# Graph network on one core: earlier node batches, the second last chunk normed in halves, a moved memory pool

## The chip, the cores and the metric

The kernel runs on one NeuronCore of a Trainium2 chip. The core has a matrix engine (PE; its weight loads are shown as PEld), a vector engine (DVE), an engine for activation functions (ACT), GpSimd (POOL), and a sync engine (SP) that here does nothing but issue DMAs. Each engine takes its own instructions in order, and they meet by semaphores. The metric is the time of one execution in microseconds, lower is better. Times are those of the device.

## The reference, cut to what matters

The input is a graph of 6250 nodes with 128 features and 200,000 edges. The edges are sorted by their destination `dst`; their sources `src` are random. One block of a graph network is added to the input:

```python
def mesh_conv(x, src, dst, ea, w1, b1, g, bt, w2, b2):
    m = concatenate([x[dst], x[src], ea], axis=-1) @ w1 + b1
    m = silu(group_norm(m, g, bt))                   # groups of 16 channels, per edge
    m = m @ w2 + b2
    return segment_sum(m, dst) / clip(count(dst), 1)[:, None]

h = relu(layernorm(x))
h = silu(group_norm(mesh_conv(h, ...first...), n1_g, n1_b)) + (silu(t_emb) @ tm_w + tm_b)
h = silu(group_norm(mesh_conv(h, ...second...), n2_g, n2_b)) + relu(layernorm(x))
q, k, v = h @ qw + qb, h @ kw + kb, h @ vw + vb      # 8 heads of 16
logits = (q[dst] * k[src]).sum(-1) / 4 + (ea @ ew + eb)
w = softmax of logits over the edges of each dst
o = segment_sum(w * v[src], dst) @ ow + ob
return x + h + group_norm(o, an_g, an_b)
```

So there are three sweeps over all edges: first convolution, second convolution, attention. Each needs for every edge a row that belongs to its source, and each sweep can start only when the node work of the sweep before is complete, since a source can be any node.

## The kernel before, in words

**Tiling.** Edges are taken 128 at a time (a tile), 8 tiles to a chunk of 1024 edges. There are 1563 tiles, so 196 chunks numbered 0 to 195, and the last chunk has only 3 tiles. Nodes are taken in 49 windows of 128. As the edges are sorted, one chunk touches a short run of nodes, and the sum of a chunk is added to two neighbouring windows of a table `flat` (named `U` in the convolutions) that stays on chip.

**One chunk of a convolution.** POOL gathers the source rows from a table `b_d` in memory, one indirect DMA for each of the 8 tiles (L718). SP loads a block of destination rows `pk` (L676) and, for two chunks at a time, a copy of the edges' positions spread over the partitions, `ohT` (L660). ACT turns `ohT` into a one-hot matrix in two passes (`compared`, L685 and L686). PE multiplies the two (`hidden`, L1174). DVE adds the gathered rows (`first`, L1181), ACT squares, DVE sums the squares of each group (L1185), ACT takes the root (L1192), and DVE the reciprocal (L1282). `normed` then does three passes on DVE (times the reciprocal L1196, times gamma L1199, plus beta L1200) and the Silu on ACT (L1201). `summed` (L1206) adds the edges up by destination on PE. `by_window` (L1211) makes two masked copies of that sum on ACT, one for each of the two windows, and `add_late` (L1216) adds them to `U` on DVE.

**Steps.** `pipeline` (L829) writes out one step per chunk. In step n the gathers of a chunk ahead are issued, chunk n gets its `first`, and an earlier chunk gets `normed` and `summed`. For one run of chunks there is one root; runs are two chunks long and become single chunks at the end. The last step takes chunks 194 and 195 together. The order on DVE, ACT, PE and SP is the order in which this function writes the instructions down, held by `in_order`; POOL is not held by it and goes ahead as far as its buffers allow (4 in the convolutions, 11 in attention).

**Batches.** While a sweep runs, windows that no later chunk touches are finished four at a time by a batch (`conv_nodes`, L950; a generator that does a little in each step). A batch divides by the count, multiplies by the second weight, normalises, takes the Silu, and multiplies by the weights of the next sweep; results go to the tables `b_d`, `a_d` (destination rows) and `kv_d` (keys and values). `plan_batches` (L375) says at which steps batches start: for the convolutions from step 81 on, every 8 steps, so 14 batches, the last at step 185. Which windows a batch takes is read from a small table that is computed on the chip from the edges. `idle` makes a batch wait some steps between its reciprocal and its transpose (6 in the first convolution, 4 in the second); the last batch of a sweep has none. In the first convolution the transpose and the Silu (`turned`, L909) stand in one step, and so do each product with the next weights and the copy of its result (L1006 and L1015).

**Ends of a sweep.** After the last chunk, `mend` (L745) reads two numbers; unless some edges or windows were left out, it does nothing, but all engines meet there. Then `last_nodes` (L1105) finishes the last 9 windows in three groups of three. Its tiles come from a pool `lastn`. Only then can the gathers of the next sweep read their table. Memory of pools that were closed is given to new pools, and the framework places the waits that this needs.

**Attention** has the same shape: gathers of keys and values (L718 on `kv_d`), products (L1384), logits (L1399 to L1405), maxima over runs of chunks for the softmax (loads of `nbs` and `nbe`, L1412), weighted sums (L1457, L1464) that are merged into `flat`.

Of the kernel before, what the change touches and what calls it, by code (L numbers as in the profile page):

```python
# [21 lines left out]
P = 128  # L22
# [7 lines left out]
G = 8  # L30
GC = 2
BN = 4
LG = 2
WN = 96
RN = 92
# [15 lines left out]
def kernel(ctx: ExitStack, tc: tile.TileContext, x, src, dst, eat, w, out):  # L51
# [323 lines left out]
    def plan_batches(i):  # L375

        ends, todo = steps_of(i)
        out, done = [], 0
        for n, now in enumerate(todo):
            done += len(now)  # L380
            if n % 8 == (4 if i == 3 else 1) and n > (40 if i == 3 else 80) and n + 6 < NCH \
                    and (i == 3 or n + 5 in ends):
                out.append((n, max(done - 3, 0)))
        return out if NWD else []
# [509 lines left out]
    class Nodes:  # L894
# [11 lines left out]
                nc.tensor.transpose(tp[:, j, :], t[:, j, :], ident)  # L906
            return tp[:, :m, :]

        def turned(self, t, m, tag="x", silu=None):  # L909

            tp = self.in_bank(t, m)
            out = self.tile(m, tag)
            if silu:
                nc.scalar.activation(out, tp, AF.Silu, bias=cols[f"{silu}_b"], scale=cols[f"{silu}_g"])
            else:
                nc.scalar.copy(out, tp)
            return out

        def times(self, tT, m, rhs):
# [27 lines left out]
    def span(w, m):  # L947
        return bass.ds(w, m) if not isinstance(w, int) else slice(w, w + m)

    def conv_nodes(b, i, w, m, idle=0, last=False):  # L950


        at = span(w, m)
# [23 lines left out]
        if i == 1 or last:  # L977
            b.inverse(A, m)
            h0T = b.in_bank(h0[:, at, :], m) if i == 2 else None
            yield  # L980
            for _ in range(idle + 2 * (idle > 0)):
                yield
            tT = b.turned(A, m, "t", silu=f"n{i}")
            if i == 2:
                nc.vector.tensor_tensor(tT, tT, h0T, ALU.add)
        else:
            b.scaled(A, m, f"n{i}_g", f"n{i}_b")
            yield
            nc.scalar.activation(A, A, AF.Silu)
# [14 lines left out]
        done = None  # L1004
        for rhs, bias, d_ in ends:
            o = b.times(tT, m, rhs)  # L1006
            if bias:
                yield
            if done:
                nc.sync.dma_start(out=rows_of(done[0], w, m), in_=done[1])  # L1010
            t = b.tile(m, "o")
            if bias:
                nc.vector.tensor_tensor(t, o, rows[bias][:, None, :].to_broadcast([P, m, D]), ALU.add)
            else:
                nc.scalar.copy(t, o)  # L1015
                yield
            done = d_, t
# [86 lines left out]

    def last_nodes(i, hx=True):  # L1105

        with tc.tile_pool(name="lastn", bufs=1) as lp, tc.tile_pool(name="lastp", bufs=6, space=PSUM) as ps:
# [28 lines left out]
    def conv(i):  # L1136
# [6 lines left out]
        with ExitStack() as es:  # L1143
# [23 lines left out]
            def over_edges(r, n):  # L1167
                return r[:, None, :].to_broadcast([P, n, D])
# [23 lines left out]
                nc.scalar.activation(sd[:, :n + also], var[:, :n + also], AF.Sqrt, bias=eps_t, scale=1.0 / HD)  # L1192
                return sd

            def normed(k):
                nc.vector.tensor_tensor(  # L1196
                    k.mt.rearrange("p t (g c) -> p t g c", c=HD), k.mt.rearrange("p t (g c) -> p t g c", c=HD),
                    k.rs.rearrange("p (t g) -> p t g", g=H)[:, :, :, None].to_broadcast([P, k.nt, H, HD]), ALU.mult)
                nc.vector.tensor_tensor(k.mt, k.mt, over_edges(gam, k.nt), ALU.mult)  # L1199
                nc.vector.tensor_tensor(k.mt, k.mt, over_edges(bet, k.nt), ALU.add)  # L1200
                nc.scalar.activation(k.mt, k.mt, AF.Silu)  # L1201

            def summed(k):
                k.u = ps_.tile([P, 3, PITCH], FP, name="u", tag="u", bufs=2)
# [13 lines left out]
            class Stage:  # L1218
# [506 lines left out]
```

## Time and profile before

| | us |
|---|---|
| median of 3 runs | 6132.63 |
| lowest and highest of them | 6124.32 and 6134.92 |
| the profiled execution, whole | 6127.41 |
| its span, first to last instruction | 6125.2 |

| engine | busy, us | share of the span |
|---|---|---|
| DVE | 4995.8 | 82% |
| POOL | 4498.1 | 73% |
| PE | 3621.9 | 59% |
| ACT | 3339.8 | 55% |

The profile has a timeline of every instruction with its start and duration, and, in brackets, how long its engine sat idle before it and which instruction of another engine ended that idle time. Groups of instructions are put together by source line; `x392` is their number, and the mean duration is in nanoseconds. The list of waits says for each pair of lines how long one waited for the other: the total, how many times, and the longest. "issue" is time in which an engine waited for nothing that the profile shows. A DMA on SP is shown at the time of its issue; "landing" is when its semaphore arrives. PEclk is the granted clock of PE, as a share of full speed.

### The profile page before, as it was taken

The numbers are of one execution on the slowest core, as the hardware profiler recorded it, in microseconds if no ns is written. First come the engines' busy times: TensorE is split into PE (matmuls) and PEld (weight loads), VectorE is DVE, ScalarE is ACT, GpSimd is POOL, SyncE is SP. The second block draws the span as 40 slices with busy tenths as digits, with TensorE's granted clock in tenths as the row PEclk, the third lists the DMA queues.
The fourth block names the chain that finished last, engine by engine and source line by source line (L and its number), as shares of the span: only waits on it lengthen the run. The fifth ranks groups of instructions, "written<-read, shape, count | busy, mean of one in ns | idle before, by whom it ended". The sixth has DMA issues, their size and how long they took to land. (4 is left out here: it accounts for less than half of the span.)

```text
span 6125.2 us, 68319 instructions
## 1 busy us (share of the span) xinstructions
PE 3621.9 (59%) x20941; PEld 3430.7 (56%) x20942; DVE 4995.8 (82%) x7118; ACT 3339.8 (55%) x5259; POOL 4498.1 (73%) x4738
## 2 busy tenths in 40 slices
PE   5565556565566455655566566655665665666665
PEld 4555555555555455555555555544555555555555
DVE  7888888888888587787888888866778888888887
ACT  5666666666666566666666666642333333333354
POOL 5777777777777577777777777757777777777774
PEclk8777777777777677776777777766777778777777
DMA  6444343444444333434444444445566666666653
GB/s 162 117 127 119 98 115 101 108 108 104 106 102 105 83 97 101 101 96 101 107 108 111 111 114 109 115 112 156 152 160 166 163 164 167 161 164 163 161 160 82
DMA packets 391220, 758.86 MB, mean 124 GB/s; under 512 B 89647, under 2 KB 256946, under 8 KB 361441
## 3 DMA queue, kind: packets, MB, share of 16 engines
q0 software_dynamic: 175056, 410.03, 26.1%
q1 hardware_dynamic: 210144, 340.73, 21.2%
q10 hardware_dynamic: 5632, 3.50, 0.2%
q8 instruction: 173, 2.83, 0.2%
q14 instruction: 215, 1.76, 0.1%
HBM read 707.34 MB, written 46.58 MB: 123 GB/s over the span
## 5 line engine op out<-in xcount | busy, mean ns | idle before, releaser
L718 POOL DMA_INDIRECT g<-b_d,src_i x3126 | 2965.1, 949 | 963.1 <-issue 917.4
L1206 PE MATMUL u<-h,oh 128*128 128x129 f32 (+1 forms) x6252 | 1282.2, 388 | 1424.2 <-ACT h L1201 1424.1
L1206 PEld LDWEIGHTS u<-h,oh 128*128 128x128 f32 x6252 | 1182.9, 291 | 1505.8 <-ACT h L1201 1501.0
L718 POOL DMA_INDIRECT g<-kv_d,src_i x1563 | 1487.8, 952 | 493.3 <-issue 445.4
L1174 PE MATMUL m<-pk,ohT 101*128 101x128 f32 x6252 | 941.6, 314 | 192.8 <-DVE h L1181 149.0
L1174 PEld LDWEIGHTS m<-pk,ohT 101*128 101x128 f32 x6252 | 910.7, 231 | 212.3 <-DVE h L1181 166.3
L1181 DVE TENSOR_TENSOR h<-m,g 128x1024 f32<-128x1024 f32 x392 | 476.4, 1215 | 512.2 <-DMA g<-b_d,src_i 500.9
L1464 PE MATMUL us<-v,oh 128*128 128x145 f32 x3126 | 585.1, 355 | 354.4 <-DVE flat L1489 309.5
L1384 PE MATMUL qe<-pk,ohT 101*128 101x136 f32 x3126 | 572.8, 354 | 369.9 <-ACT ebs L1401 361.8
L1464 PEld LDWEIGHTS us<-v,oh 128*128 128x128 f32 x3126 | 541.5, 247 | 394.3 <-DVE flat L1489 226.9
L1384 PEld LDWEIGHTS qe<-pk,ohT 101*128 101x128 f32 x3126 | 532.8, 255 | 400.0 <-ACT ebs L1401 393.5
L1201 ACT ACTIVATE h<-h 128x1024 f32<-128x1024 f32 x392 | 413.0, 1054 | 594.7 <-DVE h L1200 579.0
L1183 ACT ACTIVATE sq<-h 128x1024 f32<-128x1024 f32 x392 | 411.7, 1050 | 512.9 <-DVE h L1181 511.1
L685 ACT ACTIVATE ohT<-ohT,minus_p 96x1024 f32<-96x1024 f32 x588 | 669.2, 1138 | 16.8 <-DMA ohT<-rel_d 16.8
L686 ACT ACTIVATE ohT<-ohT 96x1024 f32<-96x1024 f32 x588 | 619.8, 1054 | 18.6
L1185 DVE TENSOR_REDUCE var<-sq 128x64 f32<-128x1024 f32 x392 | 475.3, 1212 | 99.0 <-ACT sq L1183 98.7
L1199 DVE TENSOR_TENSOR h<-h,cps 128x1024 f32<-128x1024 f32 x392 | 477.2, 1217 | 13.4
L1200 DVE TENSOR_TENSOR h<-h,cps 128x1024 f32<-128x1024 f32 x392 | 477.1, 1217 | 13.4
L741 DVE TENSOR_TENSOR oh<-cps,dm 128x1024 f32<-128x1024 f32 x392 | 474.6, 1211 | 2.3 <-PE u L1206 2.3
L1196 DVE TENSOR_TENSOR h<-h,cps 128x1024 f32<-128x1024 f32 x392 | 474.3, 1210 | 0.0
L1399 DVE TENSOR_TENSOR g<-qe,g 128x768 f32<-128x768 f32 (+1 forms) x391 | 251.2, 684 | 227.9 <-DMA g<-kv_d,src_i 227.6
L1477 ACT ACTIVATE us<-d 128x16 f32<-128x16 f32 x196 | 36.6, 187 | 649.2 <-DVE d L1473 575.3
(287 smaller groups left out, 4274.6 us busy)
## 6 DMA issues: line engine op xcount, KB each, us to landing
ohT<-rel_d SPq DMA_DIRECT2D x291, 768.0 KB
g<-b_d,src_i POOLq DMA_INDIRECT x3126, 2.5
pk<-a_d SPq DMA_DIRECT2D x588, 46.0 KB
g<-kv_d,src_i POOLq DMA_INDIRECT x1563, 3.1
ohT<-in_eat_dram SPq DMA_DIRECT2D x291, 40.0 KB
a_d<-n_o SPq DMA_DIRECT2D x28, 256.0 KB
kv_d<-n_o SPq DMA_DIRECT2D x28, 256.0 KB
n_h<-h_d SPq DMA_DIRECT2D x19, 256.0 KB
```

The source lines that it names most:

```text
L685: nc.scalar.activation(k.ohT[:WN, :], k.ohT[:WN, :], AF.Square, bias=minus_p[:WN])
L686: nc.scalar.activation(k.ohT[:WN, :], k.ohT[:WN, :], AF.Relu, bias=1.0, scale=-4.0)
L718: h = nc.gpsimd.indirect_dma_start(out=g[:, t, :table_d.shape[1]], out_offset=None, in_=table_d, in_offset=bass.IndirectOffsetOnAxis(ap=k. ...
L741: return nc.vector.tensor_tensor(k.oh[:, :k.nt, :], iota[:, None, :].to_broadcast([P, k.nt, P]), k.dm[:, :, None].to_broadcast([P, k.nt, P ...
L1174: nc.tensor.matmul(k.m[:, t, :], lhsT=lhs[:, t * P:(t + 1) * P], rhs=rhs, start=(j == 0), stop=(j == len(terms) - 1))
L1181: nc.vector.tensor_tensor(k.mt, k.m[:, :n], k.g[:, :n], ALU.add)
L1185: return lambda: nc.vector.tensor_reduce(var[:, at:at + n * H], sq[:, :n].rearrange("p t (g c) -> p (t g) c", c=HD), AX.X, ALU.add)
L1199: nc.vector.tensor_tensor(k.mt, k.mt, over_edges(gam, k.nt), ALU.mult)
L1200: nc.vector.tensor_tensor(k.mt, k.mt, over_edges(bet, k.nt), ALU.add)
L1206: nc.tensor.matmul(k.u[:, 0, :wide], lhsT=k.oh[:, t, :], rhs=k.h[:, t, :wide], start=(t == 0), stop=(t == k.nt - 1))
L1384: nc.tensor.matmul(k.qe[:, t // TB, at:at + DB], lhsT=lhs[:, t * P:(t + 1) * P], rhs=rhs, start=(j == 0), stop=(j == len(terms) - 1))
L1464: nc.tensor.matmul(k.u[:, :wide], lhsT=k.oh[:, t, :], rhs=k.v[:, t, :wide], start=(t == 0), stop=(t == k.nt - 1))
```

## The change

Four edits in one:

- The batches of both convolutions start at steps 85, 93, ..., 181: 13 instead of 14. In the first convolution the last three have no idle steps; in the last two of these the Silu stands one step after its transpose, and in the last one each copy stands one step after its product.
- In the step that ends a convolution, `normed` of chunk 194 works in two halves of 4 tiles, so that three DVE passes and a Silu become six and two.
- In the same step the masked copies of chunk 194 stand behind the Silu and the sums of chunk 195 in ACT's order, not ahead.
- `last_nodes` of the second convolution first sets aside 12632 floats per partition (`below`), so that its pool lies further up in memory. Nothing is written there.

```diff
+BELOW = 12632
@@ plan_batches
-            if n % 8 == (4 if i == 3 else 1) and n > (40 if i == 3 else 80) and n + 6 < NCH \
+            if n % 8 == (4 if i == 3 else 5) and n > (40 if i == 3 else 80) and n + (6 if i == 3 else 10) < NCH \
                     and (i == 3 or n + 5 in ends):
@@ Nodes
+        def silu_of(self, tp, m, n):
+            out = self.tile(m, "t")
+            nc.scalar.activation(out, tp, AF.Silu, bias=cols[f"{n}_b"], scale=cols[f"{n}_g"])
             return out
@@ conv_nodes
-            tT = b.turned(A, m, "t", silu=f"n{i}")
+            tp = b.in_bank(A, m)
+            if fine > 0:
+                yield
+            tT = b.silu_of(tp, m, f"n{i}")
...
             o = b.times(tT, m, rhs)
-            if bias:
+            if bias or fine > 1:
                 yield
@@ last_nodes
+        with ExitStack() as es:
+            if i == 2:
+                es.enter_context(tc.tile_pool(name="below", bufs=1)).tile([P, BELOW], FP, name="below")
+            lp = es.enter_context(tc.tile_pool(name="lastn", bufs=1))
+            ps = es.enter_context(tc.tile_pool(name="lastp", bufs=6, space=PSUM))
@@ conv: normed
-            def normed(k):
+            def normed(k, by=TPC):
+                for a in range(0, k.nt, by):
+                    n = min(by, k.nt - a)
+                    mt = k.mt[:, a:a + n]
+                    m4 = mt.rearrange("p t (g c) -> p t g c", c=HD)
+                    nc.vector.tensor_tensor(
+                        m4, m4, k.rs.rearrange("p (t g) -> p t g", g=H)[:, a:a + n, :, None].to_broadcast(
+                            [P, n, H, HD]), ALU.mult)
+                    nc.vector.tensor_tensor(mt, mt, over_edges(gam, n), ALU.mult)
+                    nc.vector.tensor_tensor(mt, mt, over_edges(bet, n), ALU.add)
+                    nc.scalar.activation(mt, mt, AF.Silu)
@@ conv: Stage.second
-                        if k.c >= NCH - SOON and self.sums:
+                        if NCH - SOON <= k.c < NCH - 1 and self.sums:
                             by_window(self.sums[0])
                             self.late.append(self.sums.pop())
                         if self.late:
                             add_late(self.late.pop(0))
-                        normed(k)
+                        normed(k, TPC // 2 if k.c == NCH - 2 else TPC)
                         summed(k)
@@ conv: Stage.batch
-                    for r in conv_nodes(nodes, i, w, BN, idle=4 if j + 1 < len(plans[i]) else 0):
+                    for r in conv_nodes(nodes, i, w, BN, idle=4 if j + (3 if i == 1 else 1) < len(plans[i]) else 0,
+                                        fine=(j + 3 - len(plans[i])) * (i == 1)):
```

The built programs differ in one more way that the diff does not tell. Before, SP loads the first `nbs`, `nbe` and `ohT` of attention in the first convolution (the profile has that `nbs` load at 890.8 us), and ACT compares them there, because their memory was free. With the pool moved up, they lie under `last_nodes`' tiles; in the changed program SP issues them behind the last writes of `last_nodes`, and ACT's four passes come after.

More of the change, by code (lines that the diff above doesn't have):

```diff
@@ L907, in in_bank, with turned @@
             return tp[:, :m, :]
-        def turned(self, t, m, tag="x", silu=None):
+        def turned(self, t, m, tag="x"):
             tp = self.in_bank(t, m)
             out = self.tile(m, tag)
[L913 to L916, printed above, removed]
+            nc.scalar.copy(out, tp)
+            return out
+        def silu_of(self, tp, m, n):
+            out = self.tile(m, "t")
+            nc.scalar.activation(out, tp, AF.Silu, bias=cols[f"{n}_b"], scale=cols[f"{n}_g"])
             return out
@@ L948, in span, with conv_nodes @@
         return bass.ds(w, m) if not isinstance(w, int) else slice(w, w + m)
-    def conv_nodes(b, i, w, m, idle=0, last=False):
+    def conv_nodes(b, i, w, m, idle=0, last=False, fine=0):
         at = span(w, m)
@@ L1105, in last_nodes @@
     def last_nodes(i, hx=True):
-        with tc.tile_pool(name="lastn", bufs=1) as lp, tc.tile_pool(name="lastp", bufs=6, space=PSUM) as ps:
+        with ExitStack() as es:
[3 more added lines that the diff above has]
+            ps = es.enter_context(tc.tile_pool(name="lastp", bufs=6, space=PSUM))
             n = NW - NWD
@@ L1193, in deviations @@
                 return sd
-            def normed(k):
[L1196 to L1201, printed above, removed]
+            def normed(k, by=TPC):
[9 more added lines that the diff above has]
+                    nc.scalar.activation(mt, mt, AF.Silu)
             def summed(k):
```

## The prediction

> **What bounds the kernel now.** I read first the busy time of each engine by stages: the first sweep, and the stretches in which POOL has no gathers to issue.
>
> ```profile
> core 0: us, PE busy (x) PEld busy (x) DVE busy (x) ACT busy (x) POOL busy (x), PEclk, DMA share, GB/s
> 56.00:2015.60 1959.60, 1154.33 (x6764) 1105.70 (x6763) 1614.84 (x1793) 1263.30 (x1545) 1483.30 (x1564) 0.74 0.43 111
> 2015.60:2069.70 54.10, 26.52 (x139) 24.05 (x137) 30.22 (x60) 28.93 (x46) 5.60 (x1) 0.68 0.09 26
> 4027.60:4076.70 49.10, 27.07 (x162) 24.90 (x162) 28.18 (x57) 17.55 (x30) 5.80 (x2) 0.75 0.25 71
> 2030.00:2050.00 20.00, 8.57 (x37) 7.67 (x36) 10.46 (x16) 7.35 (x14) 0.00 (x0) 0.50 0.01 2
> ```
>
> Then the waits of POOL, of DVE at the start of attention, and of DVE late in attention:
>
> ```profile
> POOL g L718 <- issue: 1362.7, 4472, 0.3
> DVE g L1399 <- DMA g<-kv_d,src_i: 117.5, 21, 16.0
> DVE g L1399 <- DMA g<-kv_d,src_i: 7.5, 2, 3.9
> ```
>
> A gather takes 0.95 and the next follows 0.30 later. 4472 of the 4689 gathers follow without any other cause, so a sweep is 1563 x 1.25 = 1954 us (1959.6 measured) and no faster DVE or PE shortens its middle. What can be gained lies in the two stretches without gathers, 54.1 and 49.1 us, from a sweep's last gather to the next sweep's first. A gain there reaches the end only if attention is bound by gathers: it is, since DVE waits 117.5 us for them in 4076 to 4500 and still 7.5 us in 5800 to 5950.
>
> So the sum is made over the two stretches. Their steps:
>
> ```profile
> 2014.64 0.94 POOL L718 DMA_INDIRECT g<-b_d,src_i  x1 [0.30 <-issue]
> ...
> 2035.53 1.21 DVE L1196 TENSOR_TENSOR h<-h,cps 128x1024 f32<-128x1024 f32 x1
> ...
> 2040.39 3.81 PE L1206 MATMUL u<-h,oh 128*128 128x129 f32 x16 [7.29 <-ACT h L1201]
> ...
> 2044.24 0.72 ACT L1211 ACTIVATE u<-u,mask 128x129 f32<-128x129 f32 x2 [3.90 <-PE u L1206]
> 2044.88 0.51 ACT L1201 ACTIVATE h<-h 128x384 f32<-128x384 f32 x1
> 2045.45 1.66 PE L1206 MATMUL u<-h,oh 128*128 128x129 f32 x6 [1.24 <-ACT h L1201]
> ...
> 2047.89 0.42 DVE L1216 TENSOR_TENSOR flat<-flat,u 128x258 f32 x1 [2.48 <-ACT u L1211]
> ...
> 2050.65 0.17 DVE L956 TENSOR_SCALAR n_c<-flat 128x3 f32<-128x3 f32 x1 [2.33 <-DMA wcl<-wc_d]
> ...
> 2069.71 0.95 POOL L718 DMA_INDIRECT g<-b_d,src_i  x1 [10.77 <-DMA b_d<-n_o]
> ```
> ```profile
> 4026.66 0.94 POOL L718 DMA_INDIRECT g<-b_d,src_i  x1 [0.30 <-issue]
> ...
> 4030.22 0.68 DVE L1013 TENSOR_TENSOR n_o<-nd,r_kb 128x512 f32<-128x512 f32 x1
> ...
> 4034.64 1.21 DVE L1196 TENSOR_TENSOR h<-h,cps 128x1024 f32<-128x1024 f32 x1
> ...
> 4046.97 0.42 DVE L1216 TENSOR_TENSOR flat<-flat,u 128x256 f32 x1 [2.47 <-ACT u L1211]
> 4047.31 0.69 DVE L1013 TENSOR_TENSOR n_o<-nd,r_qb 128x512 f32<-128x512 f32 x1
> ...
> 4051.69 0.31 DVE L961 COPY n_c<-cnt 128x6 f32<-128x6 f32 x3 [3.70 <-SPq L750]
> ...
> 4076.69 0.95 POOL L718 DMA_INDIRECT g<-kv_d,src_i  x1 [17.44 <-DMA pk<-a_d]
> ...
> 4088.76 1.29 DVE L1399 TENSOR_TENSOR g<-qe,g 128x768 f32<-128x768 f32 x2 [15.98 <-DMA g<-kv_d,src_i]
> ```
>
> Each stretch is: DVE's lag behind the last gather until `normed` of chunk 194; the chain through chunks 194 and 195 to the last addition; the meeting of all engines; `last_nodes`; the first gather.
>
> **Part 1, the first convolution's last batches.** The lag is 2035.53 - 2014.64 = 20.89 us; in the second convolution it is 4034.64 - 4026.66 = 7.98. The difference of 12.9 has a cause in the waits of 1964 to 2036, against the same place in the second convolution (second row), with two groups of ACT in 1964 to 2036, the last of which shows who holds ACT up:
>
> ```profile
> DVE var L1185 <- ACT sq L1183: 12.7, 5, 4.1
> DVE var L1185 <- ACT sq L1183: 0.3, 1, 0.3
> L1201 ACT ACT_TABLE_LOAD x5 | 6.4, 1283 | 0.1
> L1015 ACT COPY n_o<-nd 128x512 f32<-128x512 f32 x4 | 2.3, 586 | 16.3 <-PE nd L922 16.3
> ```
>
> In the last four steps of the batch, ACT stands at the copy of a product that PE makes only behind the sums of the chunk, some 4.1 us each; the squares are queued behind that copy and DVE waits for them. After the change the last batch starts at 181 and its copy stands a step later, when the product is long there; the batch is done some steps before the end, in which DVE regains lag. The two batches ahead of it keep the stalls in part (their idle steps are gone), but have 16 and 8 steps to regain them: DVE is busy 1614.84 of 1959.6 us, so it can regain 18% of a chunk's 10 us, 1.8 per step. The lag should become that of the second convolution: 12.4 by the waits (12.7 - 0.3), 12.9 by the lags; I take 12.6. Bounds: 8 (DVE regains only two thirds) and 14.2 (lag of 6.7, as if the 1.2 us of the second convolution's own batch work at 4030.22 and behind were gone too). What is late next is POOL's last gather, 7 to 8 us ahead.
>
> **Part 2, halves and order of ACT, in both.** From `normed` of 194 to the end of the last addition are 2048.31 - 2035.53 = 12.78, and 4047.39 - 4034.64 = 12.75. Shapes of half the size are in the batches:
>
> ```profile
> L936 DVE TENSOR_TENSOR n_A<-n_A,r_n_g 128x512 f32<-128x512 f32 x14 | 9.7, 693 | 0.5
> L989 ACT ACTIVATE n_A<-n_A 128x512 f32<-128x512 f32 x14 | 8.7, 621 | 4.3 <-DVE n_A L936 4.3
> ```
>
> New chain, from the start of `normed`: three half passes 2.1, first Silu 0.62 to 2.8, eight matmuls (half of 3.81) 1.9 to 4.7; the second half's passes end at 4.3, its Silu at 5.0, its matmuls at 6.9. Chunk 195: an addition 0.42 and three passes of 0.55 on DVE end at 6.4, its Silu (0.51, no longer behind the copies) at 6.9, its matmuls 1.66 at 8.6, copies 0.72 at 9.3, addition 0.42 at 9.8. Saved 2.95, twice: 5.9. Bounds: 1.0 each (only the 0.64 of the copies ahead of the Silu and 0.4 of overlap), 3.7 each (PE kept at a higher clock). The three extra passes cost DVE 3 x 0.16 = 0.5, within these numbers.
>
> PE's rate matters here: the windows give a granted clock of 0.50 in 2030 to 2050, and the 16 matmuls take 3.81, but 2.05 at 4010.75:
>
> ```profile
> 4010.75 2.05 PE L1206 MATMUL u<-h,oh 128*128 128x128 f32 x16 [1.48 <-ACT h L1201]
> ```
>
> The Trainium skill ("TensorE: Matmul & The Clock Gate", Part 1, the HAM clock gate) says that PE falls to half rate after an idle window of about 3.4 us, and comes back after as long a time of sustained work. By that rule PE's gap of 7.29 ahead of the sums shrinks to about 5 and stays too long, and the halves change no clock, as I have it. Were it otherwise, the second half's matmuls would take 1.0, PE would be done with chunk 194 at 6.0, chunk 195 would be the bound from 6.9, its matmuls would take 0.9, and the chain would be 9.05: 0.75 less per convolution.
>
> **Part 3, the second convolution's last batch.** With its start four steps earlier (185 to 181), its three products lie in earlier steps. On the path: the additions at 4030.22 and behind (0.68 each, of which some 1.0 is on the path to `normed`), and the one at 4047.31 with the write of its result, whose landing the meeting waits for. From the last addition's end to DVE's resuming are 4051.69 - 4047.39 = 4.30; in the first convolution, without such a write, 2050.65 - 2048.31 = 2.34. So 2.0 + 1.0 = 3.0; bounds 1.5 (the write's landing half hidden) and 3.5.
>
> **Part 4, the moved pool.** Before, attention's first gather waits for all of the last writes, as its buffers lie under `last_nodes`' tiles. In the built program its wait shrinks to the six writes of `kv_d`. Rows of the two convolutions' last issues, and the load that is moved:
>
> ```profile
> L1010 SPq DMA_DIRECT2D b_d<-n_o x3: 372/400/414, 2064.6 to 2066.7; - x3
> L1010 SPq DMA_DIRECT2D kv_d<-n_o x6: 372/372/387, 4065.5 to 4069.3; - x6
> L1022 SPq DMA_DIRECT2D h_d<-n_x x3: 453/474/475, 4071.8 to 4072.9; - x3
> L1412 SPq DMA_DIRECT2D nbs<-nbs_d x1: 314/314/314, 890.8 to 890.8; - x1
> ```
>
> At the start of the second convolution, the first gather comes 2069.71 - 2066.7 = 3.0 after the last issue of its table. 4069.3 + 3.0 to 3.8 (the old distance, from h_d's last issue at 4072.9 to 4076.69) is 4072.3 to 4073.1: 4.0 saved; bounds 0 (landings slowed by the writes in front) and 4.4.
>
> Against it stand the loads that were done at 890.8: `nbs`, `nbe` and `ohT` now go out on SP behind the last writes, and ACT's four passes behind them. `ohT` at 4076.9; the second convolution's start shows the rest:
>
> ```profile
> 2070.97 0.33 SPq L660 DMA_DIRECT2D ohT<-rel_d  x1
> ...
> 2076.59 1.15 ACT L685 ACTIVATE ohT<-ohT,minus_p 96x1024 f32<-96x1024 f32 x1 [7.88 <-DMA ohT<-rel_d]
> ```
>
> 5.6 from issue to ACT, two passes 2.2, the first products on PE 4.0: DVE's first work (L1399) about 4088.7, the same as the 4088.76 of before, though gathers began 4 us earlier. That costs nothing while DVE has the 117.5 us of waits to regain it; without this cover it would cost 4.0. POOL, with 11 buffers, does not stall at a lag of 16. `pk` loads stand on the same queue: late by the 0.3 to 0.4 of each of three issues, inside the same cover.
>
> The Trainium skill ("DMA: Bandwidth & Descriptors", "Issuing engines are not separate DMA queues") says that transfers issued by different engines share the same 16 DMA engines. That speaks against 768 KB of `ohT` beside the first gathers; by it they could land up to 6.9 us later, an estimate from 768 KB at the 111 GB/s of the first sweep. No row before shows `ohT` beside gathers of `kv_d` at a start; it is rival C.
>
> **Part 5, one batch fewer in each convolution.** It lies under gathers: 0. If it were not covered, POOL slips by 0.3 waits at most, some 0.5 in all.
>
> **Sum.** 12.6 + 5.9 + 3.0 + 4.0 = 25.5. The profiled execution takes 6127.4; less 25.5 is 6101.9. Its time is 5.2 below the median, 6132.6; less 25.5 is 6107.1. I say 6106, nearer to the median. By the bounds: 8 + 2 + 1.5 + 0 = 11.5 and 14.2 + 7.4 + 3.5 + 4.4 = 29.5, so 6103 to 6121 from the median.
>
> **Rivals.**
> (B) The squares' stall stays: the last steps of a sweep take a root for each single chunk, and ACT loads tables for root and Silu in turn; if these and not the copies set the pace, lag does not shrink. For it: five loads for the Silu in 1964 to 2036, 6.4 us, and six for the root. Against it: the second convolution has the same roots and a lag of 7.98. Gain 25.5 - 12.6 = 12.9: 6120.
> (C) `ohT` and the writes of h_d hold attention's start: part 4 gives nothing, 6111. For it: one queue, one set of DMA engines. Against it: attention's cover of 117.5.
> (D) Slower: batches that start earlier reach fewer windows. A window is ready only if no later chunk touches it; with the last batch at 181 the 40 windows are reached only if chunk 177's first destination is at least 40 x 128 = 5120. From there on `mend` does nothing; below, it finishes windows alone, with engines in turn, as long as the three groups of `last_nodes`: 2069.71 - 2050.65 = 19.1, plus another meeting, 2.3: 21.4 for each convolution, 42.8 less 25.5: 6150. Against it: by the edges that the reference draws, that destination is 5127, seven nodes on the good side.
> (E) No change that can be told: the idle steps that the two batches before the last have lost cost as much lag as they free (three batches with 12.7 of stall each, less 14.4 regained in 8 steps), and POOL, stalled from a lag of 29 on, slips: gain 25.5 less 12.6 and up to 9 more: about 6129.
>
> **How the numbers follow.** Forecast 0.70, B 0.12, C 0.07, E 0.06, D 0.05. A measurement of this kernel cannot tell less than 0.2% (12.3 us) from no change. Forecast, C and most of B (6120 is 12.9 below) are faster: 0.84; E and the rest of B within: 0.10; D and mishaps like it slower: 0.06. Range: low end 6103 less the 8.3 by which the lowest run lies under the median, 6094; high end 6121 with B's 6120, and 3 more for the median's scatter: 6124.
>
> **What the changed profile would show.** Lag of `normed`(194) of 8 us in the first convolution, and L1185's wait for squares under 2 us there; 9.8 from there to the last addition; DVE resuming 2.3 behind it in both; the first gather on `kv_d` some 3.5 behind the last write of `kv_d`; stretches without gathers of 38.5 and 39; the rest of the sweeps unchanged. Wrong it would be if a new wait of POOL stands inside a sweep, if engines run in `mend`, or if DVE no longer waits for gathers in 5800 to 5950.

## The result

| | before | changed |
|---|---|---|
| median, us | 6132.74 | 6101.1 |
| lowest and highest of 6 runs | 6124.32 and 6134.92 | 6097.21 and 6104.82 |
| the profiled execution, whole | 6127.41 | 6104.82 |

The ratio is 0.9951, with a 95% interval of 0.9940 to 0.9961: 24 to 37 us faster, 31.6 by the medians. Forecast were 6106 and a range of 6094 to 6124.

The first view is the stages of the changed kernel: the stretch, its length, the busy time of each engine with the number of instructions, and the granted clock of PE. Line numbers have moved: L719 is the gather, L1210 to L1215 are `normed`, L1220 the sums, L1225 the masked copies, L1230 the additions, L1414 attention's first product on DVE.

```profile
core 0: us, PE busy (x) PEld busy (x) DVE busy (x) ACT busy (x) POOL busy (x), PEclk, DMA share, GB/s
56.00:2019.70 1963.70, 1161.86 (x6764) 1110.95 (x6763) 1622.92 (x1790) 1268.89 (x1551) 1487.40 (x1563) 0.74 0.43 110
2019.70:2056.50 36.80, 19.19 (x105) 18.01 (x104) 19.94 (x53) 18.25 (x33) 5.63 (x2) 0.70 0.11 31
4014.30:4055.70 41.40, 24.27 (x144) 22.30 (x143) 25.50 (x53) 17.01 (x30) 5.80 (x2) 0.70 0.15 43
```

The two stretches without gathers shrank from 54.1 to 36.8 and from 49.1 to 41.4 (stretch lengths below count from the start of the last gather to the start of the next). The timeline of the first one:

```profile
2018.74 0.94 POOL L719 DMA_INDIRECT g<-b_d,src_i  x1 [0.30 <-issue]
...
2025.47 0.67 DVE L1210 TENSOR_TENSOR h<-h,cps 128x512 f32<-128x512 f32 x1
...
2028.31 4.84 PE L1220 MATMUL u<-h,oh 128*128 128x129 f32 x22 [6.51 <-ACT h L1215]
...
2031.64 0.52 ACT L1215 ACTIVATE h<-h 128x384 f32<-128x384 f32 x1 [1.34 <-DVE h L1214]
2032.19 0.72 ACT L1225 ACTIVATE u<-u,mask 128x129 f32<-128x129 f32 x2
...
2033.94 0.42 DVE L1230 TENSOR_TENSOR flat<-flat,u 128x258 f32 x1 [0.57 <-ACT u L1225]
...
2036.69 0.17 DVE L959 TENSOR_SCALAR n_c<-flat 128x3 f32<-128x3 f32 x1 [2.33 <-DMA wcl<-wc_d]
...
2056.47 0.95 POOL L719 DMA_INDIRECT g<-b_d,src_i  x1 [11.58 <-DMA b_d<-n_o]
```

And of the second one, up to attention's first product:

```profile
4013.39 0.94 POOL L719 DMA_INDIRECT g<-b_d,src_i  x1 [0.30 <-issue]
...
4020.55 0.67 DVE L1210 TENSOR_TENSOR h<-h,cps 128x512 f32<-128x512 f32 x1
...
4029.58 0.42 DVE L1230 TENSOR_TENSOR flat<-flat,u 128x256 f32 x1 [0.88 <-ACT u L1225]
4031.35 1.28 ACT L1120 ACT_TABLE_LOAD   x1 [1.80 <-DVEq L751]
...
4034.56 0.31 DVE L964 COPY n_c<-cnt 128x6 f32<-128x6 f32 x3 [4.56 <-issue]
...
4048.52 4.31 SPq L1016 DMA_DIRECT2D kv_d<-n_o  x6
...
4055.74 0.95 POOL L719 DMA_INDIRECT g<-kv_d,src_i  x1 [13.64 <-ACT n_x L914]
...
4058.84 0.34 SPq L1427 DMA_DIRECT2D nbs<-nbs_d  x1
...
4074.27 1.29 DVE L1414 TENSOR_TENSOR g<-qe,g 128x768 f32<-128x768 f32 x2 [14.33 <-DMA g<-kv_d,src_i]
```

Each term of the prediction's sum can be read off these rows (last gather, start of `normed` of 194, end of the last addition, DVE's resuming, next gather):

| term | before, us | changed, us | gain | forecast |
|---|---|---|---|---|
| lag, first convolution | 20.89 | 6.73 | 14.16 | 12.6 |
| chain, first convolution | 12.78 | 8.89 | 3.89 | 2.95 |
| meeting and last nodes, first convolution | 21.40 | 22.11 | -0.71 | 0 |
| lag, second convolution | 7.98 | 7.16 | 0.82 | 1.0 |
| chain, second convolution | 12.75 | 9.45 | 3.30 | 2.95 |
| meeting, second convolution | 4.30 | 4.56 | -0.26 | 2.0 |
| last nodes, second convolution | 25.00 | 21.18 | 3.82 | 4.0 |
| sum | | | 25.02 | 25.5 |

The two profiled executions differ by 22.3 in span. The three sweeps, first to last gather, together took 5878.05 before and 5884.60 changed, 6.6 more; the tail behind the last gather took 85.80 and 82.15, 3.65 less. The sweeps' share is scatter of the gathers themselves: their durations add up to 8.5 more, and what lies between them to 2.0 less. In two other kernels of the experiments (order_alone and no_late_steps_3), the sweeps took 5883.4 and 5876.7 with the same gathers. So the medians' 31.6 stands against 25.0 in the stretches and 3.7 in the tail; the rest is within the interval.

In the experiments the kernel before took 6134 to 6136 us on two chips (the fast pace below), as in the result, and 7930 to 7942 on three others (the slow pace), so times are compared at one pace only, and across the two only local stretches, where the text says so.

### The profile page after: what moved, and what is told of

Its sections match the earlier page's. It is cut to its first block, busy times and chain, and to the rows that moved or that the text cites. A ratio compares the mean times of both kernels' runs of the same rounds, so it can differ in the third digit from the quotient of the medians.

```text
span 6102.9 us, 68120 instructions
## 1 busy us (share of the span) xinstructions
PE 3585.6 (59%) x20869; PEld 3392.7 (56%) x20870; DVE 4987.4 (82%) x7096; ACT 3337.4 (55%) x5252; POOL 4503.7 (74%) x4738
## 5 line engine op out<-in xcount | busy, mean ns | idle before, releaser
L719 POOL DMA_INDIRECT g<-b_d,src_i x3126 | 2969.1, 950 | 964.2 <-issue 918.8
L1220 PE MATMUL u<-h,oh 128*128 128x129 f32 (+1 forms) x6252 | 1274.5, 386 | 1424.1 <-ACT h L1215 1424.0
L1220 PEld LDWEIGHTS u<-h,oh 128*128 128x128 f32 x6252 | 1176.3, 290 | 1505.1 <-ACT h L1215 1501.4
L719 POOL DMA_INDIRECT g<-kv_d,src_i x1563 | 1489.5, 953 | 490.1 <-issue 447.2
L1191 DVE TENSOR_TENSOR h<-m,g 128x1024 f32<-128x1024 f32 x392 | 476.6, 1216 | 545.6 <-DMA g<-b_d,src_i 518.1
L1479 PE MATMUL us<-v,oh 128*128 128x145 f32 x3126 | 568.7, 348 | 365.5 <-DVE flat L1504 324.0
L1479 PEld LDWEIGHTS us<-v,oh 128*128 128x128 f32 x3126 | 525.2, 240 | 405.4 <-DVE flat L1504 233.2
L1215 ACT ACTIVATE h<-h 128x1024 f32<-128x1024 f32 (+2 forms) x394 | 413.4, 1049 | 605.3 <-DVE h L1214 589.8
L1213 DVE TENSOR_TENSOR h<-h,cps 128x1024 f32<-128x1024 f32 (+2 forms) x394 | 477.4, 1212 | 13.6
L1214 DVE TENSOR_TENSOR h<-h,cps 128x1024 f32<-128x1024 f32 (+2 forms) x394 | 477.3, 1212 | 13.5
L1210 DVE TENSOR_TENSOR h<-h,cps 128x1024 f32<-128x1024 f32 (+2 forms) x394 | 474.1, 1203 | 0.0
L1414 DVE TENSOR_TENSOR g<-qe,g 128x768 f32<-128x768 f32 (+1 forms) x391 | 251.0, 683 | 225.1 <-DMA g<-kv_d,src_i 222.6
```

What stands on the lines that cost most here:

```text
L719: h = nc.gpsimd.indirect_dma_start(out=g[:, t, :table_d.shape[1]], out_offset=None, in_=table_d, in_offset=bass.IndirectOffsetOnAxis(ap=k. ...
L1191: nc.vector.tensor_tensor(k.mt, k.m[:, :n], k.g[:, :n], ALU.add)
L1213: nc.vector.tensor_tensor(mt, mt, over_edges(gam, n), ALU.mult)
L1214: nc.vector.tensor_tensor(mt, mt, over_edges(bet, n), ALU.add)
L1220: nc.tensor.matmul(k.u[:, 0, :wide], lhsT=k.oh[:, t, :], rhs=k.h[:, t, :wide], start=(t == 0), stop=(t == k.nt - 1))
L1479: nc.tensor.matmul(k.u[:, :wide], lhsT=k.oh[:, t, :], rhs=k.v[:, t, :wide], start=(t == 0), stop=(t == k.nt - 1))
```

## The experiments

**Part 1 without its late steps** (the changed kernel, but the Silu and copies of the first convolution's last batches stand where they stood before). The question was whether the earlier start alone does it (rival B in its weak form), or the copy behind PE's products is the stall.

```diff
-                    for r in conv_nodes(..., fine=(j + 3 - len(plans[i])) * (i == 1)):
+                    for r in conv_nodes(..., fine=0):
```

> The changed kernel without the later Silu and copy, by itself in a call, since the call with a single kernel beside the one before took 6132 and the calls with two and four took 7900. Theory: where the kernel before takes 6130, the stall of 4 us in four steps comes back in steps 185 to 190, the lag to normed of 194 is about 12 instead of 6.7, the stretch without gathers about 43 instead of 37.7, the time falls by 21 to 26 instead of 26 to 31. Rival: the start four steps earlier is enough, lag 7, stretch 38, no difference to the changed kernel.

Measured at the fast pace: 6111.09 against 6133.87 before, ratio 0.9965 (0.9952 to 0.9979), 13 to 29 us faster. The lag is 18.3, between the 20.9 of before and the 6.7 of the changed kernel: worse than both the theory's 12 and the rival's 7. The stretch is 50.8 us. Waits of DVE in 1964 to 2040, first of this kernel and then of the changed kernel:

```profile
DVE var L1195 <- ACT sq L1193: 8.4, 3, 4.3
DVE cps L1296 <- ACT sd L1202: 2.9, 6, 0.7
```
```profile
DVE cps L1296 <- ACT sd L1202: 3.4, 6, 1.1
...
DVE var L1195 <- ACT sq L1193: 0.5, 2, 0.3
```

The groups of ACT's copies, of this kernel (1900 to 2036) and of the changed kernel (1900 to 2030), say who held ACT:

```profile
L1021 ACT COPY n_o<-nd 128x512 f32<-128x512 f32 x2 | 1.2, 586 | 10.9 <-PE nd L925 10.9
```
```profile
L1021 ACT COPY n_o<-nd 128x512 f32<-128x512 f32 x2 | 1.1, 566 | 0.0
```

With the copy in the step of its product, ACT waits 5.5 us for each of the two, and DVE waits for the squares. With the copy a step later the same two copies wait for nothing. So of the 14.2 of lag, 2.6 come from the earlier start together with the lost idle steps, and 11.6 from the late steps on top of these; the earlier start with its idle steps kept was not run. Why the theory's 12 was too low is seen in the lag of each chunk's first addition behind its last gather (worked out from the timeline's rows of L1191 and L719): at chunk 189 it is 12.2 in this kernel and 3.0 before, at 190 20.6, then it falls by some 1.5 a chunk to 14.5 at 195. It is 13.8 already at 182, where the changed kernel has 4.7, and still 8.4 at 187, where that has 3.7: without the late Silu, the batch before leaves lag that is not regained in the eight steps to the next. The forecast's regaining of 1.8 a step was near the 1.5; the lag to start from was not zero.

Two runs at the slow pace came ahead of it:

> The changed kernel, but the Silu and the copies of the first convolution's last batches stand in the step of their transpose and product again (the starts at 85 to 181 and the lost idle steps stay). Theory: the stall of 4 us in four steps comes back, in steps 185 to 190, and about 7 of its 12.6 are regained by the end: lag of normed of 194 some 12 instead of 6.7, 5 to 6 us slower than the changed kernel. Rival: the start four steps earlier is enough, lag 7, no difference.

> The changed kernel without the later Silu and copy once more, for a chip on which the kernel before takes 6130. Theory: the stall of 4 us in four steps comes back in steps 185 to 190, lag to normed of 194 about 12 instead of 6.7, some 5 us slower than the changed kernel (gain over before 21 to 26 instead of 26 to 31). Rival: the earlier start alone is enough, lag 7, no difference.

They took 7860.99 and 7860.49 against 7937.32 and 7941.61, ratios 0.9908 (0.9881 to 0.9935) and 0.9904 (0.9887 to 0.992). There the lag is 29.2 and 29.1 us without the late steps, and 31.5 to 31.7 in the four runs with them (batches_alone, its two repeats and no_meeting), far above both the theory's 12 and the rival's 7: inconclusive for this question.

**Parts 1, 3 and 5 alone** (the kernel before, with the changed batches only):

```diff
-            if n % 8 == (4 if i == 3 else 1) and ... and n + 6 < NCH \
+            if n % 8 == (4 if i == 3 else 5) and ... and n + (6 if i == 3 else 10) < NCH \
...
+            tp = b.in_bank(A, m)
+            if fine > 0:
+                yield
...
```

> The kernel before with parts 1, 3 and 5 alone: the batches from 85 to 181, with the idle steps and the later Silu and copy of the change; no halves, order of ACT and pool as before. Theory: the lag from the last gather to normed of 194 is 6.7 in the first convolution (20.9 before) and 7.2 in the second (8.0 before), the chains stay at 12.8; time falls by 15. On the meeting of the second convolution the two reasons differ: if DVE was held by the landing of the last write (the prediction), it resumes 2.3 after its last addition, and the fall is 17; if it is held by its own code being loaded, 4.5, and the fall is 15.

> The same kernel as batches_alone (parts 1, 3 and 5 alone), on another occasion: the chip of that call took 7937 us for the kernel before, with PE without instructions in long stretches, so its stretches between sweeps say little of the ones predicted. Where the kernel before takes 6130: lag to normed of 194 6.7 in the first convolution (20.9 before) and 7.2 in the second (8.0), chains of 12.8, the meeting of the second convolution 4.5 by the loading of DVE's code or 2.3 by the landing of a write; time falls by 15 (17). Where PE is again without instructions: the fall is 74, as in that call.

> Parts 1, 3 and 5 alone once more, for a chip on which the kernel before takes 6130. Theory: lag to normed of 194 6.7 in the first convolution (20.9 before) and 7.2 in the second (8.0), chains 12.8, meeting of the second convolution 4.3 to 5.0 as in the two runs on slow chips (no write is left there, so it is DVE's code that loads): time falls by 15. If the landing of the write had been the wait: meeting 2.3, time falls by 17.

All three fell on the slow pace: 7863.11 against 7937.32, 7856.67 against 7930.2, 7861.07 against 7941.61; ratios 0.9918 (0.9894 to 0.9941), 0.9909 (0.9883 to 0.9936), 0.9894 (0.9877 to 0.991). 74 to 81 us faster is five times the 15 expected for the fast pace, and comes from elsewhere: the first sweep is shorter by 40 and the second by 19 than in the kernel with part 2 alone, first run of each. At that pace POOL waits for DVE (the last section has the rows), so a batch need no longer be covered by the gathers; what share the number of batches has, and what share their place, was not separated. For the meeting the three runs are plain: the second convolution has no write of `a_d` left in its last steps there, and DVE resumes 5.00, 4.98 and 5.38 after its last addition.

**The meeting of the second convolution.** The prediction put 2.0 us there on the landing of a write. The changed kernel has no such write, and DVE resumed after 4.56, while ACT was through the same meeting 1.35 after the last addition (4031.35 in the timeline above). What moves in 4029 to 4036 is in the DMA view of the changed kernel:

```profile
DMA packets 7, 0.07 MB, mean 11 GB/s; under 512 B 0, under 2 KB 0, under 8 KB 0
## 3 DMA queue, kind: packets, MB, share of 16 engines
q14 instruction: 5, 0.04, 2.0%
q8 instruction: 2, 0.03, 1.7%
```

Only instructions are loaded, and DVE's wait has no releaser but "issue". The same stretch of the kernel before, 4046 to 4053, has as many instruction packets, and the write beside them:

```profile
q1 hardware_dynamic: 528, 0.26, 13.1%
q8 instruction: 2, 0.03, 2.3%
q14 instruction: 5, 0.04, 1.7%
```

There ACT is through only 4.07 after the last addition, released by SP, which waits for the write:

```profile
4051.46 1.28 ACT L1110 ACT_TABLE_LOAD   x1 [4.52 <-SPq L750]
```

The write thus held the meeting before. But the same instruction packets move in both kernels, so they do not tell why DVE is no earlier without the write; DVE's own branch does. These are DVE's second branch of the meeting and its first semaphore instructions behind it, in the kernel before and then in the changed one (durations in ns, then the first and last start in us):

```profile
L750 DVEq COMPARE_BRANCH  x1: 41/41/41, 4048.2 to 4048.2; - x1
L750 DVEq EVENT_SEMAPHORE  x3: 49/50/50, 4048.8 to 4049.0; - x3
```
```profile
L751 DVEq COMPARE_BRANCH  x1: 41/41/41, 4030.8 to 4030.8; - x1
L751 DVEq EVENT_SEMAPHORE  x2: 50/50/50, 4033.2 to 4033.3; - x2
```

Before, DVE is past its branch in 0.53 and then stands at the semaphores until the write has landed, at 4050.66. In the changed kernel no write is left, but DVE needs 2.42 for the branch, and then passes its 12 semaphore instructions, 1.17, without a wait. PE shows the reverse at its own branch, 3.66 before and 0.38 in the changed kernel. The split of DVE is the same in every trace: 0.53 in the six with the write (before, order_alone, halves_alone and the three with part 4 alone), 2.30 to 3.20 in the seven with the changed batches and the meeting.

The experiment takes the meeting of the second convolution away; with it goes the work for edges and windows left out, of which these edges have none.

```diff
-            mend(1, left, pools, lambda w: batch_at_once(nodes, i, w))
+            if i == 1:
+                mend(1, left, pools, lambda w: batch_at_once(nodes, i, w))
```

> The changed kernel without the meeting of the second convolution (mend is not written out there, and with it goes the work for edges and windows left out, of which there are none with these edges). Theory (DVE's 4.56 at the meeting is the meeting itself and the loading of its code behind the branch): DVE goes on within 0.5 of its last addition, the time falls by 4 against the changed kernel. Rival (DVE waits there for something else, a write or its sums): 4 us of wait remain at DVE's first copy, no change.

It ran at the slow pace: 7847.83 against 7941.61 before, ratio 0.9879 (0.9862 to 0.9895), 12.7 less than the kernel without late steps beside it, which differs from it in two edits. Its timeline, where the last addition and the next work of DVE stand, and the DMA view of 4979 to 4985:

```profile
4979.79 0.42 DVE L1230 TENSOR_TENSOR flat<-flat,u 128x256 f32 x1 [0.39 <-ACT u L1225]
4980.25 1.50 DVE L966 TENSOR_TENSOR n_x<-flat,n_c 128x384 f32<-128x384 f32 x3
```
```profile
DMA packets 0, 0.00 MB, mean 0 GB/s; under 512 B 0, under 2 KB 0, under 8 KB 0
```

DVE goes on after 0.04 us, and no instructions are loaded there. So the 4.56 are the meeting with its branches, not a write. What the meeting is worth in whole time is not told by this run, since the changed kernel itself was not timed at that pace. From the last addition's end to the first gather of attention are 22.77 us, and 25.74 in the changed kernel (local stretches of the two paces); the difference is 3.0 and not 4.6; ACT now loads its table for the root (1.28) behind the variances, at 4987.44, where the meeting had hidden it. The Trainium skill ("Runtime: NRT & Kernel Launch", Instruction fetch mechanics) says that a taken branch to a page that is not held makes the engine fetch that page by DMA before it goes on; DVE's 2.42 at the branch beside the instruction packets agrees with it, though the trace does not say which packet was DVE's, nor why the same branch takes 0.53 in the other programs.

**Part 2, its two halves.** The order of ACT alone, on the kernel before:

```diff
-                        if k.c >= NCH - SOON and self.sums:
+                        if NCH - SOON <= k.c < NCH - 1 and self.sums:
```

> The kernel before with the half of part 2 that moves ACT's order alone: the masked copies of chunk 194 stand behind the Silu of chunk 195; normed whole as before. Theory (the halves matter, the order little): the Silu of 195 is ready 4 us earlier, but its matmuls stand behind the 3.8 of chunk 194's on PE; PE then goes on without the gap of 1.2, so the chain of 12.8 becomes 11.6 in both convolutions. Rival: the order is the main gain and the chain falls to 10 or less; the halves then only shift PE's start.

One execution at the fast pace: 6132.15 against 6135.78, too near for single executions to tell apart. The chains are 11.04 and 10.82, so the order gives 1.7 and 1.9, more than the 1.2 expected and short of the rival's 2.8. The timeline of the first convolution:

```profile
2039.52 1.21 DVE L1196 TENSOR_TENSOR h<-h,cps 128x1024 f32<-128x1024 f32 x1
...
2044.38 4.98 PE L1206 MATMUL u<-h,oh 128*128 128x129 f32 x22 [7.29 <-ACT h L1201]
...
2050.14 0.42 DVE L1216 TENSOR_TENSOR flat<-flat,u 128x258 f32 x1 [0.74 <-ACT u L1211]
```

The 22 matmuls of both chunks now run in one piece, 4.98 where 3.81 and 1.66 were before: the gap of 1.2 is gone, and 0.5 more, little of it by the clock, whose granted share was 0.53 in 2044.3 to 2049.4. The order with the halves, on the kernel before:

```diff
-                        normed(k)
+                        normed(k, TPC // 2 if k.c == NCH - 2 else TPC)
```

> The kernel before with part 2 alone: normed of chunk 194 in halves and the Silu of chunk 195 ahead of the masked copies; batches and pools as before. Theory: the chain from normed of 194 to the end of the last addition, 12.78 and 12.75 us before, becomes 8.9 and 9.5 as in the changed kernel, since its 22 matmuls run without a gap; the stretches without gathers shrink from 55.1 and 50.0 to 51.2 and 46.7, and the time falls by 7.2. Rival: the gain needs the changed batches too (PE free of their products), and the chain becomes 9.8 or longer: 6 or less.

This fell on the slow pace, 7929.28 against 7937.32, ratio 0.9997 (0.9982 to 1.0011). The chains are local, and are 9.60 and 9.59: 3.2 saved without the changed batches, so these are not needed for it. Of the 3.3 to 3.9 in the changed kernel the order has about 1.8 and the halves, by difference, 1.4 to 2.1.

**Part 4 alone** (the pool moved, on the kernel before):

```diff
+            if i == 2:
+                es.enter_context(tc.tile_pool(name="below", bufs=1)).tile([P, BELOW], FP, name="below")
```

> The kernel before with part 4 alone: last_nodes' pool of the second convolution further up. Theory: attention's first gather comes 3.3 after the last write of kv_d is issued (7.4 before), the stretch without gathers shrinks from 50.0 to 45.9, DVE's first product of attention comes 18 us after that gather instead of 12, which its waits for gathers cover; time falls by 4.1. Rival C of the prediction: attention gives the 4.1 back, time falls by less than 1.

> The same kernel as pool_alone (part 4 alone), on another occasion. Where the kernel before takes 6130: attention's first gather 3.3 after the last write of kv_d (7.4 before), DVE's first product 18 us after that gather, the time falls by 4.1; by rival C by less than 1. Where PE is without instructions, no change, as in the first call.

> Part 4 alone once more, for a chip on which the kernel before takes 6130. Theory: nodes' stretch (DVE's resuming to attention's first gather) 21 instead of 25.0, DVE's first product of attention some 10 us later behind that gather (22 to 24 on the slow chips, 12.1 before), covered by the 117.5 us that DVE waits for gathers: time falls by 4. Rival C: DVE never regains it, no change or slower by up to 6.

At the slow pace, three times: 7937.78 against 7937.32, 7930.03 against 7930.2, 7943.35 against 7941.61, ratios 1.0002 (0.999 to 1.0014), 0.9999 (0.9982 to 1.0016), 0.9999 (0.9987 to 1.0011): no change. The local stretch from DVE's resuming to the first gather is 20.57, 22.82 and 22.96, against 26.03, 25.67, 27.25 and 26.13 in the runs at that pace without the moved pool: 3 to 7 us earlier. But DVE's first product came 22.5, 23.9 and 26.0 us behind that gather (11.7 to 12.4 without), so from its resuming to that product are 43.1, 46.7 and 48.9 us instead of 37.7 to 39.1: DVE began later, and at that pace POOL waits for DVE. At the fast pace the changed kernel shows the same at the start, 18.5 behind the gather, and these are DVE's waits for gathers in 4055 to 4500, and in 5780 to 5930:

```profile
DVE g L1414 <- DMA g<-kv_d,src_i: 116.3, 22, 14.3
DVE g L1414 <- DMA g<-kv_d,src_i: 4.5, 2, 4.1
```

The cover is there: 116.3 us. From attention's first gather to the end are 2048.5 before and 2049.3 with the order alone, 2047.2 in the changed kernel and 2043.4 without the late steps: with the moved pool no charge for DVE's lateness is seen. The stretch from DVE's resuming to the first gather is 25.00 and 25.29 in the two kernels without the moved pool at the fast pace, 21.18 and 21.21 in the two with it. That part 4 is worth its 3.8 there is read from these stretches; part 4 alone was not timed at the fast pace.

## Why the prediction was right

**What bounds.** Right at this pace: the sweeps stayed as long as the gathers take, and what was gained in the stretches arrived at the end.

**The sum.** 25.0 against 25.5 is closer than its terms: Parts 1 and 2 gave 2.9 more than forecast, the meeting 2.3 less, and the other terms 1.1 less. That these cancel is luck. The median fell by 31.6, more than the 29.5 that the upper bounds add up to; 6101 lies below the 6103 of the bounds and inside the range only by what was added there for scatter.

**Part 1.** The mechanism was right (ACT at the copy, PE's product behind the chunk's sums, squares queued behind): the wait for squares in the window fell from 12.7 to 0.5 (1964 to 2025), and no_late_steps_3 brings it back. The size was 12.6 forecast and 14.16 measured, almost the upper bound: the lag went below the second convolution's old one, since that had its own batch in its last steps, which the bound had named. It held that the two batches ahead of the last "have 16 and 8 steps to regain" their stalls. In the changed kernel they do (3.7 at chunk 187), but this hangs on the late Silu: in no_late_steps_3 the lag is 8.4 there and then piles up to 20.6. The start at 181, with the lost idle steps, was worth 2.6. Rival B fell: the roots and table loads are all still there, and lag is 6.7.

**Part 2.** 2.95 forecast, 3.89 and 3.30 measured. PE began 2.84 and 2.83 after the start of `normed` (2.8 forecast), and from PE's end to the chain's end are 1.21 and 1.20 (1.2 forecast). All of the difference is PE's own run: 5.8 forecast, 4.84 and 5.42 measured. Two terms in it were mis-sized. The last 6 matmuls were counted at 1.66, which they take as a piece of their own; with half the clock from end to end the whole run takes 5.57 and the chain 9.60 (halves_alone, first convolution). The rest is PE's clock, of which the prediction said "the halves change no clock, as I have it". Two windows in PE's first run of the changed kernel, one in its second, and one of halves_alone (columns as in the first view, the granted clock third from the end):

```profile
2028.31:2031.73 3.42, 3.42 (x14) 3.17 (x15) 3.19 (x6) 0.72 (x2) 0.00 (x0) 0.50 0.00 0
2031.73:2033.15 1.42, 1.36 (x10) 0.97 (x8) 0.21 (x1) 1.11 (x3) 0.00 (x0) 1.00 0.00 0
4023.38:4028.52 5.14, 5.14 (x22) 4.80 (x22) 3.43 (x7) 1.84 (x4) 0.00 (x0) 0.50 0.00 0
2551.63:2557.20 5.57, 5.57 (x22) 4.94 (x22) 3.62 (x7) 1.84 (x4) 0.00 (x0) 0.50 0.00 0
```

The clock rose 3.42 us into the run in the first convolution, 5.14 into it in the second, when the run was nearly done, and not at all in halves_alone. By the Trainium skill ("TensorE: Matmul & The Clock Gate", Part 1, the HAM clock gate), the full clock returns after some 3.4 us of sustained work, counted in windows that run freely and do not start with the kernel. The two runs of the changed kernel agree with it, and in the kernel before the clock stayed at 0.50 through both pieces and the gap. Of the 12 chains of this form in six traces at either pace, eight take 9.37 to 9.62 and four 8.88 or 8.89, so the 8.89 is in part luck of where the clock rises. The prediction's lower figure of 9.05 is near to 8.89, but it had put that on a shorter gap ahead of the run, which stayed at 6.51.

**Part 3.** Its second half failed, 2.0 forecast and -0.26 measured: "the one at 4047.31 with the write of its result, whose landing the meeting waits for". That was right of the kernel before: the write landed at 4050.66, the engines passed the rest of the meeting only behind it, and without it ACT is through 1.35 after the last addition (4.07 before). What was put at nothing is DVE's own branch. It took 0.53 before, and takes 2.42 in the changed kernel, where the step ahead of it holds other instructions; at 0.53 DVE would have resumed after about 2.7, an estimate from these rows, and 1.6 of the 2.0 would have come. Why the branch takes longer in that program is open. The comparison with the first convolution's 2.34 held only for a branch of 0.56, which DVE has there in all traces. The additions' 1.0 was right (0.82).

**Part 4.** Right: 4.0 forecast, 3.8 measured; the gather follows 3.3 after the last write of `kv_d` is issued (4052.5 to 4055.74). The row names ACT's copy n_x as releaser, but that only ended near by. The semaphores in the trace show the landings: the sixth write of `kv_d` landed at 4054.66, 1.08 ahead of the gather. Before, the gather stood until the last write of `h_d` landed at 4075.62, 1.07 ahead of it, though `kv_d` had landed at 4071.56: 4.06 of waiting for other tables. `ohT` and its helpers were later than forecast for DVE, 18.5 behind the first gather where 16 was expected, and were covered as forecast; rival C fell at this pace. At the slow pace that cover is gone, and part 4 gives nothing.

**Part 5.** Zero was right here. Its price without cover, "some 0.5 in all", was not tested by itself; where POOL waits for DVE, the changed batches together shorten the sweeps by some 40 and 19.

**What the sum left out.** -0.71 in the first convolution's last nodes: PE's first transposes there begin 1.78 after DVE's resuming (1.11 before), cause not shown; the same stretch took 18.6 to 21.5 in the other kernels. And 3.65 in the tail, of which the cause stays open: the two kernels at the fast pace with the moved pool have 82.2 and 82.4, the two without 85.8 and 85.4. Rivals D and E did not come about: no engine has work in `mend`, and POOL has no new wait of more than 0.7 inside a sweep.

## What to carry to other kernels

An in-order engine that copies a product in the step that makes it inherits every queue ahead of that product; here one step of delay took away a stall of 4 to 5.5 us each time, and moving the whole batch earlier without it 2.6 in all. Before pricing the removal of a wait, look at what each engine does in that stretch besides waiting: here DVE's branch over a skipped piece of program cost 0.53 us in one program and 2.3 to 3.2 in another, which took the whole gain. A gain in a stretch where the bounding engine sits idle is worth its full size only as long as that engine is still the bound afterwards; on chips of another pace the same kernel had another bound, and only the changed batches counted clear of the noise.

## What was not expected of the hardware

At the slow pace PE stands still for long with nothing to wait for. These are the waits of PE of the kernel with part 4 alone (first run), and its POOL's; in the kernel before at the fast pace, PE waited 14.2 us for issue at L1174 in all, and POOL's waits of a gather for DVE inside a sweep are 0.3 each.

```profile
PE u L1211 <- issue: 791.6, 485, 12.9
PE m L1179 <- issue: 620.1, 429, 35.8
```
```profile
POOL g L719 <- issue: 1372.5, 4391, 6.6
POOL g L719 <- DVE h L1186: 961.4, 165, 24.5
```

In the timeline of the kernel with part 2 alone PE begins one instruction, weight loads counted, each 0.70 us for some 5 to 19 us, and then runs at its usual pace again; this comes back mostly every 20 to 40 us of the stretch looked at, 130 to 700. Matmuls themselves are no slower there. Three rows of it:

```profile
1027.22 0.37 PE L1210 MATMUL u<-h,oh 128*128 128x129 f32 x1 [0.82 <-issue]
1028.62 0.37 PE L1210 MATMUL u<-h,oh 128*128 128x129 f32 x1 [1.03 <-issue]
1029.32 0.37 PE L1210 MATMUL u<-h,oh 128*128 128x129 f32 x1 [0.33 <-issue]
```

What sets the pace is open. That instructions came late to PE is not shown: this kernel has 173 and 217 instruction packets (queues q8 and q14), order_alone at the fast pace 173 and 216, and their mean durations agree to 0.02 us. The slow pace went with several changed kernels on the chip beside the one before (three chips), the fast one with a single one (two chips); whether the number of programs or the chip decides was not told apart.
